# Last batch's attention products on VectorE alone, rows normalized on ScalarE, and loads of rows and expert weights in turn

## The chip, the cores and the metric

The kernel runs on one core of a Trainium2 chip. The metric is the device time of one execution in microseconds. The engines are TensorE (PE: matmuls, with its weight loads PEld), VectorE (DVE), ScalarE (ACT), GpSimd (POOL) and SyncE (SP, which only starts DMAs here). Each takes its instructions in the order in which the program was built, and waits for the others by semaphores.

## The reference

The reference is one layer with cross attention and a mixture of experts, in fp32. B is 4, S 512, the context 1024, D 256, with 16 heads of 16.

```python
x = x + xattn(layernorm(x), ctx, ctx, mask, w_q, w_k, w_v, w_o)   # 16 heads, rope
x = x + ffn(layernorm(x), ln1, ln2, qkv, proj, router, w1, w2)
...
# ffn: hidden_states is (S=256 there, B=4); here dimension 0 has 4 entries and dimension 1 has 512
qkv = einsum('sbh,oh->sbo', ln1_out, qkv_weight)      # 16 query heads, 4 key and value heads
scores = where(causal, einsum('sbhd,tbhd->bhst', q, k) * scale, min)
hidden_after_attn = hidden_states + softmax(scores) @ v @ proj
x = layernorm2(hidden_after_attn)
gate = softmax(x @ router); top_probs, top_idx = top_k(gate, 2)     # of 8 experts
h_mid = gelu(x @ w1[e]); expert_out = h_mid @ w2[e]                 # 256 -> 512 -> 256
out = hidden_after_attn + sum of the two chosen experts, weighted by their gates
```

The second attention runs over the first dimension, which has 4 entries: token t of batch b attends, in each of 16 heads, to token t of batches 0 to b. It is called the inner attention below, and it is no work for matmuls: it is elementwise products with sums over 16 numbers. Batch 3, the last, has the most: four products of q with keys, and four of weights with values.

## The kernel before

**Stages.** Cross attention runs first, batch after batch, in 128 steps of a plan: PE computes scores (L1133 for the maxima, L1154 for the exponentials) and sums (L1172). The second half of the layer is cut into eight halves, `half(b, h)` for batch b and 256 of its 512 tokens. A half is a Python generator: normalization, transposition (L294), q, k, v (psq, L443), inner attention, transposition (psa), projection (psp, L537), residual h2 (L544), second normalization (rows, L557), transposition (psx), router (psl, L569), the choice of two experts (L586 to L608), a placing (psr, L617 to L621: a running count gives each token a row in its expert's table; indices at L638), and four indirect DMAs by POOL (L648) that scatter 2 x 128 rows into `table` in DRAM, twice each. The halves of batches 0 and 1 and most of batch 2 are spread over the plan's steps. What is left of batch 2, and batch 3, run after cross attention, interleaved with the experts.

**Experts.** Tokens are handled in 39 tiles of up to 128 rows of one expert. Lists of tiles are planned as batches become ready: list a has tiles 0 to 8 (after batch 1), b tiles 9 to 16 (after batch 2), c tiles 17 to 25 and d tiles 26 to 38 (after batch 3). A tile needs 128 rows of the table (132.5 KB, SP at L799), its expert's w1 (512 KB, SP at L830, a ring of 8 places, w1 being loaded seven tiles ahead), and w2, which is resident. On PE a tile is psu (16 matmuls, L1432, with a gelu on ScalarE, L1441), psxe (2 transpositions of the next tile's rows, L1414, copied by ScalarE, L1417) and psy (8 matmuls, L1450, copied by ScalarE at L1461). POOL scatters its result (L1464, `given_rows`) once or twice. Where to is computed on VectorE by `gates` (L813 to L820) for a group of a list's tiles: 9 tiles for a, 8 for b, 2 and 7 for c, 13 for d.

**The order after cross attention.** The loop at the end of the kernel goes over the tiles. In round n it emits psu of tile n-1 in two parts, psxe of tile n, and psy of tile n-2 in two parts. Between two of these pieces `others` resumes the generators in `going`: the remaining halves, the plans of lists, the final sums. A generator's `yield "D1.5|G2.4"` tells what it has just emitted: 1.5 us on VectorE beside 2.4 on GpSimd (P, A, D, G are PE, ScalarE, VectorE, GpSimd). `passed` adds that to clocks of the four engines, and the generator is resumed when PE's clock has got to the end of that work (with "!" at the end of the text) or to 2.5 us before. So these texts set the order of all instructions of this stage; no engine departs from it.

**Loads of rows and w1.** `load_list` runs when a list is planned. It goes through all its tiles, and for each tile calls `load_w1` (which issues w1 loads as far as seven tiles beyond the tiles used) and then issues the load of that tile's rows. The first row load of a list waits for the scatters of its batch (`scattered`). After each tile's gelu `load_w1` is called again.

**The last batch's inner attention.** In `half` with b = 3, products alternate: batches 0 and 2 on GpSimd, 1 and 3 on VectorE (L484 for q with keys into `pr`, L509 for weights with values into `pv`); VectorE reduces the scores (L495) and the largest (L496), ScalarE does the exponential (L500) with a change of its function table before it and one back before the next gelu, VectorE sums, divides (L502 to L504) and adds the four products over their batch index by one reduction (L520). For batch 2 the additions are instructions of their own on VectorE (L527).

Of the kernel before, what the change touches and what calls it, by code (L numbers as in the profile page):

```python
# [173 lines left out]
def kernel(  # L174
# [229 lines left out]
    def products_of(name, b):  # L404
        if b < B - 1:
            return k2.tile([P, B - 1, HALF, DK], F32, tag="pr", name=name, bufs=1)
        return late["pool"].tile([P, B, HALF, DK], F32, tag="prlast", name=name, bufs=2)

    def half(b, h):


        n = f"{b}_{h}"
        last = b == B - 1
        mv, *rest = norms_of(b, h)
        yield "D1.7 G1.1"
        both, back, minus = norms_end(b, h, mv, *rest)
        t0 = 2 * h
        if last:
# [17 lines left out]
        if h == 0:  # L436
            keys[b] = keep.tile([P, NQT, KVH * DK], F32, tag=f"keys{b}", name=f"keys{b}")
            values[b] = keep.tile([P, NQT, KVH * DK], F32, tag=f"values{b}", name=f"values{b}")
        q = k2.tile([P, 2, D], F32, tag="q", name=f"q{n}", bufs=1)
        for i in range(2):  # L440
            ps = bank(f"psq{n}_{i}")
            for c in range(KC):
# [23 lines left out]
        def grouped(x):  # L466
            return x.rearrange("p (k r) d -> p k r d", r=REP)

        if b == 0:

            yield
            yield
            yield
            at = k2.tile([P, HALF, DK], F32, tag="at", name=f"at{n}", bufs=1)
            nc.gpsimd.tensor_copy(grouped(at), of_batch(values, 0))
            yield
        else:

            def engine(j):
                return nc.vector if last and j % 2 else nc.gpsimd  # L480

            pr = products_of(f"pr{n}", b)
            for j in range(b + 1):
                engine(j).tensor_tensor(  # L484
                    grouped(pr[:, j]),
                    grouped(q.rearrange("p i (h d) -> p (i h) d", d=DK)),
                    of_batch(keys, j),
                    ALU.mult,
                )
            yield "D1.5|G2.4"  # L490
            sc = k2.tile([P, B, HALF], F32, tag="sc", name=f"sc{n}")[:, 0 : b + 1, :]
            top = k2.tile([P, HALF], F32, tag="top", name=f"top{n}")
            by_head = sc.rearrange("p j n -> p n j")
            over = [P, b + 1, HALF]
            nc.vector.tensor_reduce(sc, pr[:, 0 : b + 1], AX.X, ALU.add)  # L495
            nc.vector.tensor_reduce(top, by_head, AX.X, ALU.max)  # L496
            nc.vector.tensor_tensor(sc, sc, top.unsqueeze(1).to_broadcast(over), ALU.subtract)
            if last:
                yield "D3!"
            nc.scalar.activation(sc, sc, AF.Exp, scale=SCALE)  # L500
            yield "A2.9"
            nc.vector.tensor_reduce(top, by_head, AX.X, ALU.add)  # L502
            nc.vector.reciprocal(top, top)
            nc.vector.tensor_tensor(sc, sc, top.unsqueeze(1).to_broadcast(over), ALU.mult)  # L504
            yield "D1"
            at = k2.tile([P, HALF, DK], F32, tag="at", name=f"at{n}", bufs=1)
            pr = products_of(f"pv{n}", b)
            for j in range(b + 1):
                engine(j).tensor_tensor(  # L509
                    grouped(pr[:, j] if j or last else at),  # L510
                    of_batch(values, j),
                    sc[:, j, :]
                    .rearrange("p (k r) -> p k r", r=REP)
                    .unsqueeze(3)
                    .to_broadcast([P, 2 * KVH, REP, DK]),
                    ALU.mult,
                )
            if last:
                yield "D1.5|G2.4"
                nc.vector.tensor_reduce(  # L520
                    at.rearrange("p n d -> p (n d)"),
                    pr.rearrange("p j n d -> p (n d) j"),
                    AX.X,
                    ALU.add,
                )
            for j in range(1, 1 if last else b + 1):
                (nc.vector if b == 2 else nc.gpsimd).tensor_tensor(at, at, pr[:, j], ALU.add)  # L527
            yield "D2.2!"
        aT = wide(f"aT{n}")
        rows_of = at.rearrange("p (i h) d -> p i (h d)", i=2)  # L530
        transposed(aT, lambda i: rows_of[:, i, :], f"psa{n}")
# [18 lines left out]
        nc.vector.tensor_scalar(v, mv2[:, :, 1], EPS, None, ALU.add)  # L550
        r = power_of(v, 2, "m", f"m{n}")
        nc.gpsimd.tensor_tensor(xt[:, b, t0 : t0 + 2, :], xt[:, b, t0 : t0 + 2, :], h2, ALU.add)
        yield "D1.4 G0.7"
        newton(v, r, 2, "m", f"m{n}")
        rows = k2.tile([P, 2, ROW], F32, tag="rows", name=f"rows{n}")
        for i in range(2):
            nc.vector.tensor_scalar(  # L557
                rows[:, i, 0:D], h2[:, i, :], mv2[:, i, 0:1], r[:, i : i + 1], ALU.subtract, ALU.mult
            )
        yield "D1.4!"  # L560
        xT = wide(f"xT{n}")
        transposed(xT, lambda i: rows[:, i, :], f"psx{n}", 2)
        yield "P0.5 A1.1!"
# [18 lines left out]
        if last:  # L582
            yield "P1 D0.4!"
        nc.scalar.activation(lg, lg, AF.Exp)
        yield "A2.8"
        nc.vector.tensor_reduce(m, lg, AX.X, ALU.add)  # L586
        nc.vector.reciprocal(m, m)
        nc.vector.tensor_tensor(lg, lg, m.to_broadcast(small), ALU.mult)
# [197 lines left out]
    def load_list(name, T, memory):  # L786

        hot, at, beyond = planned["c" if name == "d" else name]
        at0 = FIRST if name == "d" else 0
        of = slice(at0, at0 + T)  # L790
        rows = memory.rearrange("p (t w) -> p t w", w=ROW)
        first, end = {"a": (0, 16), "b": (16, 24), "c": (24, 32), "d": (0, 0)}[name]
        for i in range(T):
            n = at0 + i
            tiles.append((name, i, rows[:, i, :], at[0:1, 1, n : n + 1], at[0:1, 2, n : n + 1]))
            if i:
                load_w1()
            row = nc.sync.value_load(at[0:1, 0, n : n + 1], min_val=0, max_val=E * TOKENS - P)
            inst = nc.sync.dma_start(out=rows[:, i, :], in_=table[bass.ds(row, P), :])  # L799
            if i == 0:  # L800
                after(inst, scattered[first:end])
                load_w1()
        number[name] = memory_of(name, "number", [P, T, 1], I32)
        lists[name] = rows, hot[:, of, :], None if beyond is None else beyond[:, of]

    def gates(name, i0, i1):

        rows, hot, beyond = lists[name]
        of = slice(i0, i1)
        T = i1 - i0  # L810
        g8 = k2.tile([P, LISTS[2] - FIRST, E], F32, tag="g8", name=f"g8{name}{i0}", bufs=1)[:, 0:T, :]
        to = k2.tile([P, LISTS[2] - FIRST], F32, tag="to", name=f"to{name}{i0}", bufs=1)[:, 0:T]
        nc.vector.tensor_tensor(g8, rows[:, of, D : D + E], hot[:, of, :], ALU.mult)  # L813
        nc.vector.tensor_reduce(to, g8, AX.X, ALU.add)
        nc.vector.scalar_tensor_tensor(
            to, to, -float(TOKENS), rows[:, of, D + E], ALU.mult, ALU.add
        )
        if beyond is not None:
            nc.vector.tensor_tensor(to, to, beyond[:, of], ALU.add)
        nc.vector.tensor_copy(number[name][:, of, 0], to)  # L820

    w1_of = []
    used = [0]

    def load_w1():

        while len(w1_of) < len(tiles) and len(w1_of) < used[0] + W1RING - (used[0] > 0):
            expert = nc.sync.value_load(tiles[len(w1_of)][4], min_val=0, max_val=(E - 1) * KC)
            w1_of.append(turn(w1_ring).rearrange("p (c f) -> p c f", f=F))
            nc.sync.dma_start(  # L830
                out=w1_of[-1],
                in_=moe_w1.rearrange("e (c p) f -> p (e c) f", p=P)[:, bass.ds(expert, KC), :],
            )
# [591 lines left out]
    def expert_up(k, part):  # L1425

        if part == 0:
            ps_of[k] = pss.tile([P, F], F32, tag="s", name=f"psu{k}")
        for f in range(2 * part, 2 * part + 2):
            of = slice(f * P, (f + 1) * P)  # L1430
            for c in range(KC):
                nc.tensor.matmul(  # L1432
                    ps_of[k][:, of],
                    w1_of[k][:, c, of],
                    xT_of[k][:, c, :],
                    start=(c == 0),
                    stop=(c == KC - 1),
                )
        if part == 1:
            h_of[k] = turn(h_ring)  # L1440
            nc.scalar.activation(h_of[k], ps_of[k], AF.Gelu_apprx_tanh)  # L1441
            used[0] += 1
            load_w1()

    def expert_down(k, c):
        if c == 0:
# [58 lines left out]
    early = SECOND + EARLY_ALL  # L1505


    ENDS = {"a": (FIRST,), "b": (LISTS[1],), "c": (2, FIRST), "d": (LISTS[2] - FIRST,)}

    def second():  # L1510

# [29 lines left out]


    clock = dict.fromkeys("PADG", 0.0)
    HOP, EARLY = 0.15, 2.5
    going = {}

    def passed(work):

        at = clock["P"]
        for together in work.rstrip("!").split():
            ends = []
            for item in together.split("|"):
                clock[item[0]] = max(clock[item[0]], at) + float(item[1:])
                ends.append(clock[item[0]])
            at = max(ends) + HOP
        return at if work.endswith("!") else at - EARLY

# [137 lines left out]
```

## Time and profile before

| What | Value |
|---|---|
| Runs (3) | 857.05 us median, 854.38 to 857.39 |
| The profiled execution | 852.59 us, span 850.9 us |
| PE busy, share of the span | 802.8 us, 94% |
| VectorE, ScalarE, GpSimd busy | 542.4 us (64%), 454.0 us (53%), 287.9 us (34%) |
| Mean granted clock of PE | 0.984 of full speed |
| Last piece of cross attention (psd, L854) | starts at 640.67 us |
| psxe of tile 17, the first of list c | starts at 737.65 us |
| Last psy (tile 38) | starts at 835.99 us |

Times are microseconds from the start of the span unless "ns" stands there. A line of a list of groups or of a timeline names line, engine, operation, what is written from what, shapes and count. In a timeline the first two numbers are start and duration, merged over the count; brackets hold the idle time of the engine just before, and what ended it. SPq is SP's queue of DMA starts. Matmuls are pipelined, so a busy PE is not a PE at its peak.

### The profile page before, as it was taken

The numbers are of one execution on the slowest core, as the hardware profiler recorded it, in microseconds if no ns is written. First come the engines' busy times: TensorE is split into PE (matmuls) and PEld (weight loads), VectorE is DVE, ScalarE is ACT, GpSimd is POOL, SyncE is SP. The second block draws the span as 40 slices with busy tenths as digits, with TensorE's granted clock in tenths as the row PEclk, the third lists the DMA queues.
The fourth block names the chain that finished last, engine by engine and source line by source line (L and its number), as shares of the span: only waits on it lengthen the run. The fifth ranks groups of instructions, "written<-read, shape, count | busy, mean of one in ns | idle before, by whom it ended". The sixth has DMA issues, their size and how long they took to land.

```text
span 850.9 us, 15007 instructions
## 1 busy us (share of the span) xinstructions
PE 802.8 (94%) x5335; PEld 420.5 (49%) x5335; DVE 542.4 (64%) x1296; ACT 454.0 (53%) x920; POOL 287.9 (34%) x445
## 2 busy tenths in 40 slices
PE   5999999999999999999999999999999979896993
PEld 4553433333443334444334333433337869786993
DVE  5686666766776677886777778888755694400033
ACT  2325656656565655656665565555575654342441
POOL 6815342001353300164562201223213654342531
PEclk9999999999999999999999999999999999997998
DMA  7239101607000000000000023000071451478655
GB/s 231 59 96 308 56 1 58 173 22 208 2 2 1 25 2 1 1 33 20 2 1 1 1 79 120 26 23 6 25 231 62 152 170 41 145 229 305 207 160 164
DMA packets 55642, 73.38 MB, mean 86 GB/s; under 512 B 5721, under 2 KB 40569, under 8 KB 55568
## 3 DMA queue, kind: packets, MB, share of 16 engines
q1 hardware_dynamic: 49968, 61.08, 23.6%
q0 software_dynamic: 4080, 10.07, 3.3%
q10 hardware_dynamic: 1520, 1.27, 0.5%
q8 instruction: 43, 0.70, 0.3%
q14 instruction: 31, 0.25, 0.1%
HBM read 42.88 MB, written 30.75 MB: 87 GB/s over the span
## 4 chain that ended last, share of the span: by engine, by line
PE 72%; issue 9%; DVE 9%; POOL 5%; DMA 2%; ACT 1%; SPq 1%; POOLq 0%; ACTq 0%; DVEq 0%
PE psm L1133 29%; PE av L1172 13%; PE psv L1047 3%; PE psk L1014 3%; POOL given_rows L1464 3%; PE psu L1432 3%; DVE mx L1140 3%; PE pss L1154 2%; PE psq L443 2%; PE psy L1450 2%; PE psp L875 2%; PE psqt L1113 2%; PE pskt L1035 2%; PE psq L1093 2%; PE psp L537 1%
## 5 line engine op out<-in xcount | busy, mean ns | idle before, releaser
L1140 DVE TENSOR_REDUCE mx<-psm 128x1 f32<-128x512 f32 x512 | 326.7, 684 | 133.5 <-PE pss L1154 119.2
L1162 ACT ACTIVATE ex<-pss 128x512 f32<-128x512 f32 x512 | 277.3, 596 | 204.0 <-PE pss L1154 197.0
L1133 PE MATMUL psm<-kT_odd,shared 32*128 32x512 f32 x512 | 152.7, 639 | 1.1 <-DVE mx L1140 0.9
L1154 PE MATMUL pss<-qt,shared 32*128 32x512 f32 x512 | 152.0, 639 | 0.0
L1154 PE MATMUL pss<-qt,kT_odd 32*128 32x512 f32 x512 | 145.9, 644 | 0.5 <-ACT ex L1162 0.5
L1133 PE MATMUL psm<-shared 32*128 32x512 f32 x512 | 144.5, 639 | 1.0 <-ACT shared L1121 0.9
L1172 PE MATMUL av<-ex,vaug 128*32 128x512 f32 (+1 forms) x872 | 106.6, 558 | 0.6 <-ACT oraw L1181 0.6
L1432 PE MATMUL psu<-shared 128*128 128x128 f32 x624 | 81.2, 283 | 11.3 <-DMA shared<-in_moe_w_dram 9.2
L1432 PEld LDWEIGHTS psu<-shared 128*128 128x128 f32 x624 | 78.5, 197 | 15.6 <-issue 9.6
L979 POOL TENSOR_TENSOR shared<-shared 128x256 f32<-128x256 f32 x44 | 33.3, 757 | 140.8 <-ACT shared L1022 108.4
L1133 PEld LDWEIGHTS psm<-kT_odd,shared 32*128 32x128 f32 x512 | 43.8, 183 | 72.3 <-DVE mx L1140 29.4
L1450 PE MATMUL psy<-shared 128*128 x312 | 77.2, 389 | 0.6 <-ACT shared L1461 0.5
L1133 PEld LDWEIGHTS psm<-shared 32*128 32x128 f32 x512 | 43.6, 183 | 66.7 <-DVE mx L1140 27.5
L1450 PEld LDWEIGHTS psy<-shared 128*128 128x128 f32 x312 | 58.0, 197 | 8.7 <-ACT shared L1461 0.9
L1172 PEld LDWEIGHTS av<-ex,vaug 128*32 128x32 f32 x872 | 17.5, 108 | 83.7 <-issue 79.6
L1441 ACT ACTIVATE shared<-psu 128x512 f32<-128x512 f32 x39 | 23.4, 599 | 59.9 <-PE psu L1432 58.1
L1154 PEld LDWEIGHTS pss<-qt,kT_odd 32*128 32x128 f32 x512 | 42.7, 184 | 7.5 <-ACT ex L1162 3.0
L648 POOL DMA_INDIRECT table<-rows,index x32 | 32.4, 1013 | 41.1 <-DVE index L638 23.6
L1496 DVE SCALAR_TENSOR_TENSOR y<-y,gate,xt 128x256 f32<-128x256 f32 x16 | 7.7, 481 | 58.6 <-DMA y<-given_rows 58.6
L981 POOL TENSOR_TENSOR shared<-shared 128x128 f32<-128x128 f32 x88 | 44.6, 528 | 0.0
L1154 PEld LDWEIGHTS pss<-qt,shared 32*128 32x128 f32 x512 | 44.0, 183 | 0.6 <-ACT ex L1162 0.6
L268 POOL TENSOR_TENSOR rm<-vm,power 128x2 f32<-128x2 f32 x8 | 5.7, 712 | 102.2 <-DVE vm L550 102.2
(300 smaller groups left out, 1055.6 us busy)
## 6 DMA issues: line engine op xcount, KB each, us to landing
shared<-in_moe_w_dram SPq DMA_DIRECT2D x47, 512.0 KB, 4.5
table<-zeros SPq DMA_DIRECT2D x8, 2120.0 KB, 17.8
shared<-in_ctxT_dram SPq DMA_DIRECT2D x8, 512.0 KB, 4.2
y<-given_rows SPq DMA_DIRECT2D x12, 256.0 KB, 4.0
shared<-table SPq DMA_DIRECT2D x18, 132.5 KB, 3.6
xt<-in_x_dram SPq DMA_DIRECT2D x4, 512.0 KB, 7.8
rows_d<-table SPq DMA_DIRECT2D x13, 132.5 KB, 2.2
out_dram<-y SPq DMA_DIRECT2D x6, 256.0 KB, 2.2
```

Source lines behind the costliest of these rows:

```text
L648: inst = nc.gpsimd.indirect_dma_start(out=table, out_offset=bass.IndirectOffsetOnAxis(ap=index, axis=0), in_=rows, in_offset=None, bounds_ ...
L979: engine.tensor_tensor(a, src, over(f[:, 0:DK]), ALU.mult)
L981: engine.tensor_tensor(r[:, :, i::2], src[:, :, 1 - i :: 2], over(f[:, DK + i : 2 * DK : 2]), ALU.mult,)
L1014: nc.tensor.matmul(ps[:, 0:D], context(b, kc, c), wk_sb[:, c, :] if b else unpaired(wkp, c), start=(c == 0), stop=(c == KC - 1),)
L1047: nc.tensor.matmul(ps[:, 0:D], context(b, kc, c), wv_sb[:, c, :], start=(c == 0), stop=(c == KC - 1),)
L1133: nc.tensor.matmul(ps, q1[m][rows, t * P : (t + 1) * P], kT[b % 2][rows, g, h * 512 : (h + 1) * 512], start=True, stop=True,)
L1140: nc.vector.tensor_reduce(mx[m][:, t, j, h : h + 1], ps, AX.X, ALU.max)
L1154: nc.tensor.matmul(ps, kT[b % 2][rows, g, kc * P : (kc + 1) * P], q2[m][rows, :], start=True, stop=True,)
L1162: nc.scalar.activation(ex[m, kc, j], ps, AF.Exp, scale=SCALE)
L1172: nc.tensor.matmul(av[m][32 * j : 32 * j + 32, over], vaug[(b * NKC + kc) % VRING][:, 4 * g + j, :], x[:, over], start=(kc == 0), stop=(kc ...
L1432: nc.tensor.matmul(ps_of[k][:, of], w1_of[k][:, c, of], xT_of[k][:, c, :], start=(c == 0), stop=(c == KC - 1),)
L1450: nc.tensor.matmul(ps_of[k], h_of[k][:, f * P : (f + 1) * P], w2_sb[:, bass.ds(weights_of[k] + f * D, D)], start=(f == 0), stop=(f == F // ...
```

## The change

The diff has four parts.

1. In the last batch every product of the inner attention is on VectorE (L484, L509), and the four value products are added by three additions in place of the reduction at L520. The q tile of the last batch has two buffers of its own.
2. The rows of the last batch (L557) are normalized by ScalarE as an activation with scale r and bias -mean x r; VectorE computes that bias.
3. `load_list` puts row loads into a queue `unloaded`; `load_tiles`, in place of `load_w1`, issues before each w1 load one row load (first four tiles of a list other than d) or two. `gates` issues what is missing for its group. The groups of gates are smaller: c in 2, 3 and 4 tiles, d in 4, 4 and 5.
4. The texts of the yields have other durations, and there is a new letter E: ScalarE's work with a table load of 1.3 us ahead of it, and 1.3 us behind it that delay only ScalarE's next work.

```diff
+    def of_half(shape, tag, n, last):
+        if last:
+            return late["pool"].tile(shape, F32, tag=f"{tag}last", name=f"{tag}{n}", bufs=2)
+        return k2.tile(shape, F32, tag=tag, name=f"{tag}{n}", bufs=1)
...
-        yield "D1.7 G1.1"
+        yield "D2 G1.2"
...
-        q = k2.tile([P, 2, D], F32, tag="q", name=f"q{n}", bufs=1)
+        q = of_half([P, 2, D], "q", n, last)
...
-            def engine(j):
-                return nc.vector if last and j % 2 else nc.gpsimd
+            engine = nc.vector if last else nc.gpsimd
...
-                engine(j).tensor_tensor(
+                engine.tensor_tensor(
...
-            yield "D1.5|G2.4"
+            yield "D2.8"
...
-            yield "A2.9"
+            yield "E0.3"
...
-                    grouped(pr[:, j] if j or last else at),
+                    grouped(pr[:, j] if j else at),
...
             if last:
-                yield "D1.5|G2.4"
-                nc.vector.tensor_reduce(
-                    at.rearrange("p n d -> p (n d)"),
-                    pr.rearrange("p j n d -> p (n d) j"),
-                    AX.X,
-                    ALU.add,
-                )
-            for j in range(1, 1 if last else b + 1):
-                (nc.vector if b == 2 else nc.gpsimd).tensor_tensor(at, at, pr[:, j], ALU.add)
-            yield "D2.2!"
+                yield "D2.8"
+            for j in range(1, b + 1):
+                (nc.vector if b >= 2 else nc.gpsimd).tensor_tensor(at, at, pr[:, j], ALU.add)
+            yield "D2.1!"
...
+        if last:
+            away = k2.tile([P, 2], F32, tag="away", name=f"away{n}")
+            nc.vector.scalar_tensor_tensor(away, mv2[:, :, 0], -1.0, r, ALU.mult, ALU.mult)
+            yield "D0.8!"
         for i in range(2):
-            nc.vector.tensor_scalar(
-                rows[:, i, 0:D], h2[:, i, :], mv2[:, i, 0:1], r[:, i : i + 1], ALU.subtract, ALU.mult
-            )
-        yield "D1.4!"
+            of = slice(i, i + 1)
+            if last:
+                nc.scalar.activation(
+                    rows[:, i, 0:D], h2[:, i, :], AF.Identity, bias=away[:, of], scale=r[:, of]
+                )
+            else:
+                nc.vector.tensor_scalar(
+                    rows[:, i, 0:D], h2[:, i, :], mv2[:, i, 0:1], r[:, of], ALU.subtract, ALU.mult
+                )
+        yield "A1.2!"
...
-        yield "A2.8"
+        yield "E0.3"
...
-            if i:
-                load_w1()
-            row = nc.sync.value_load(at[0:1, 0, n : n + 1], min_val=0, max_val=E * TOKENS - P)
-            inst = nc.sync.dma_start(out=rows[:, i, :], in_=table[bass.ds(row, P), :])
-            if i == 0:
-                after(inst, scattered[first:end])
-                load_w1()
+            others_ = scattered[first:end] if i == 0 else ()
+            unloaded.append((name, i, rows[:, i, :], at[0:1, 0, n : n + 1], others_))
         number[name] = memory_of(name, "number", [P, T, 1], I32)
+        load_tiles()
...
+        while any(u[0] == name and u[1] < i1 for u in unloaded):
+            load_row()
...
-    def load_w1():
+    def load_row():
+        name, _, rows, at, others_ = unloaded.pop(0)
+        row = nc.sync.value_load(at, min_val=0, max_val=E * TOKENS - P)
+        inst = nc.sync.dma_start(out=rows, in_=table[bass.ds(row, P), :])
+        after(inst, others_)
+
+    def load_tiles():
 
         while len(w1_of) < len(tiles) and len(w1_of) < used[0] + W1RING - (used[0] > 0):
+            name, i = tiles[len(w1_of)][0:2]
+            for _ in range(1 if name != "d" and i < 4 else 2):
+                if unloaded:
+                    load_row()
             expert = nc.sync.value_load(tiles[len(w1_of)][4], min_val=0, max_val=(E - 1) * KC)
...
-    ENDS = {"a": (FIRST,), "b": (LISTS[1],), "c": (2, FIRST), "d": (LISTS[2] - FIRST,)}
+    ENDS = {"a": (FIRST,), "b": (LISTS[1],), "c": (2, 5, FIRST), "d": (4, 8, LISTS[2] - FIRST)}
...
-    HOP, EARLY = 0.15, 2.5
+    HOP, EARLY, LOAD = 0.15, 2.5, 1.3
...
             for item in together.split("|"):
-                clock[item[0]] = max(clock[item[0]], at) + float(item[1:])
-                ends.append(clock[item[0]])
+                engine, takes = item[0], float(item[1:])
+                if engine == "E":
+
+                    engine, takes = "A", takes + LOAD
+                clock[engine] = max(clock[engine], at) + takes
+                ends.append(clock[engine])
+                if item[0] == "E":
+                    clock[engine] += LOAD
```

More of the change, by code (lines that the diff above doesn't have):

```diff
@@ L508, in half @@
             for j in range(b + 1):
-                engine(j).tensor_tensor(
-                    grouped(pr[:, j] if j or last else at),
+                engine.tensor_tensor(
+                    grouped(pr[:, j] if j else at),
                     of_batch(values, j),
@@ L552, in half @@
         nc.gpsimd.tensor_tensor(xt[:, b, t0 : t0 + 2, :], xt[:, b, t0 : t0 + 2, :], h2, ALU.add)
[L553 removed]
+        yield "D1.4 G0.8"
         newton(v, r, 2, "m", f"m{n}")
         rows = k2.tile([P, 2, ROW], F32, tag="rows", name=f"rows{n}")
+        if last:
+            away = k2.tile([P, 2], F32, tag="away", name=f"away{n}")
+            nc.vector.scalar_tensor_tensor(away, mv2[:, :, 0], -1.0, r, ALU.mult, ALU.mult)
+            yield "D0.8!"
         for i in range(2):
[L557 to L560 removed]
+            of = slice(i, i + 1)
[8 more added lines that the diff above has]
+        yield "A1.2!"
         xT = wide(f"xT{n}")
@@ L820, in gates @@
         nc.vector.tensor_copy(number[name][:, of, 0], to)
-    w1_of = []
+    w1_of, unloaded = [], []
     used = [0]
-    def load_w1():
+    def load_row():
[4 more added lines that the diff above has]
+    def load_tiles():
         while len(w1_of) < len(tiles) and len(w1_of) < used[0] + W1RING - (used[0] > 0):
+            name, i = tiles[len(w1_of)][0:2]
+            for _ in range(1 if name != "d" and i < 4 else 2):
+                if unloaded:
+                    load_row()
             expert = nc.sync.value_load(tiles[len(w1_of)][4], min_val=0, max_val=(E - 1) * KC)
@@ L1442, in expert_up @@
             used[0] += 1
-            load_w1()
+            load_tiles()
     def expert_down(k, c):
```

## The prediction

> **What bounds the kernel now.** I read the page's 40 slices first. TensorE (PE) is at nine tenths nearly everywhere; the weak slices are the last ten, and the granted clock dips there too.
>
> ```profile
> PE   5999999999999999999999999999999979896993
> ...
> PEclk9999999999999999999999999999999999997998
> ```
>
> Then the list of waits, for PE alone from 640 to 840 us, the stage after attention. It says which wait ends last, how long in total, how often, and the longest.
>
> ```profile
> PE psu L1432 <- DMA shared<-in_moe_w_dram: 9.2, 1, 9.2
> PE psa L294 <- DVE at L520: 4.0, 2, 3.0
> PE psxe L1414 <- DMA shared<-table: 2.4, 1, 2.4
> ```
>
> Three things hold PE: one w1 load (9.2), the last batch's inner attention on VectorE (4.0), and the first rows of list c (2.4). The timeline of PE around the largest (start, duration, then in brackets the idle time before it):
>
> ```profile
> 760.15 1.95 PE L1432 MATMUL psu<-shared 128*128 128x128 f32 x16
> 761.94 0.38 PE L1414 MATMUL psxe<-ident,shared 128*128 128x128 f32 x2
> 762.16 1.89 PE L1450 MATMUL psy<-shared 128*128 x8
> 773.28 3.75 PE L1432 MATMUL psu<-shared 128*128 128x128 f32 x16 [9.23 <-DMA shared<-in_moe_w_dram]
> 776.82 0.63 PE L1414 MATMUL psxe<-ident,shared 128*128 128x128 f32 x2
> 777.25 2.52 PE L1450 MATMUL psy<-shared 128*128 x8
> ```
>
> A tile (psu, psxe, psy) recurs every 3.73 us; tile 23's psu, due at 763.9, comes at 773.28, and its round then takes 6.32 instead of 3.73, because the granted clock is 0.50 from 770 to 778 (table of windows). So this hole costs 9.23 + 2.59 = 11.8. Its cause is in the queue of SP:
>
> ```profile
> 735.48 0.34 SPq L799 DMA_DIRECT2D shared<-table  x1
> ...
> 749.10 4.43 SPq L799 DMA_DIRECT2D shared<-table  x4
> 754.31 14.46 SPq L799 DMA_DIRECT2D rows_d<-table  x13
> 769.60 12.35 SPq L830 DMA_DIRECT2D shared<-in_moe_w_dram  x10
> ```
>
> From 749.1 to 768.8 SP issues 17 loads of rows, 1.11 each (14.46/13), that nobody needs yet, and the w1 of tile 23 stands behind them.
>
> **The loads (part one of the change).** The same 22 loads of rows and 22 of w1 are issued for lists c and d, in another order: one row to one w1 for four tiles, then two rows to one w1. A pair costs SP 1.11 + 1.24 = 2.35 (12.35/10 = 1.24 for a w1), a triple 3.46. With row c0 at t, w1 of tiles 17 to 20 are out by t + 9.4, that of tile 23 by t + 19.8; before it was t + 34.1 (735.48 to 769.60). Tile 23's psu is due about t + 28. A triple per 3.73 us is what PE eats, so the lead holds, and the rows are used up at w1 29. The channel carries it: a triple and two result scatters are 512 + 265 + 256 KB per 3.73 us, 277 GB/s; 778 to 782 moved 357. So the hole goes: minus 11.8. What is late next is nothing on SP: the slots of w1's ring fall free 8 tiles earlier. Smaller groups of gates (three more groups of five VectorE instructions at 0.2, 3 us in all) lie in VectorE's idle time. List b's rows now stand between w1 loads that wait for slots; by the walk below the last is out by about 681, VectorE wants them at 693: nothing, and 1 us for each that SP is late beyond that.
>
> **Inner products on VectorE alone.** GpSimd loses 8 products (two groups each of L484 and L509: 3.45, 2.70, 2.50, 2.06, 10.7 us), VectorE gets these 8 and 6 additions, and loses two reductions of L520. Its rows:
>
> ```profile
> 667.84 2.37 DVE L484 TENSOR_TENSOR pr<-q,keys 128x512 f32<-128x512 f32 x2 [0.97 <-ACT q L450]
> ...
> 680.53 3.74 DVE L520 TENSOR_REDUCE at<-pv 128x512 f32<-128x2048 f32 x1 [0.94 <-POOL pv L509]
> 684.18 1.29 DVE L484 TENSOR_TENSOR pr<-q,keys 128x512 f32<-128x512 f32 x2
> ```
>
> The same pair takes 2.37 while GpSimd multiplies (667.89 to 671.34) and 1.29 while it does not: 0.64 alone, 1.19 beside. After the change GpSimd has no products then, so I take 0.64, bounds 0.64 and 1.19. An addition of that size, L527 in batch 2, took 0.69 to 1.53; I take 0.69, the quiet one. A half thus has 2.6 (products) + 2.29 + 0.7, the exponential, 1.05, 2.6 + 2.1, that is 11.3 of VectorE against 16.4 that half 0 took from 667.84 to 684.27, waits and exponential included.
>
> **The order.** The built order of each engine is the same up to tile 1's psu (648.10), and different until psu16; what PE does in between is the same work. On ScalarE the first normalization (L425) moves behind psu4's gelu, from 657.9 to about 665.4; the transposition of attention outputs moves from after psu7 to within psu11 for half 0, from before psu10 to before psu12 for half 1; and the last placing (L617 to L621) from the middle of psu14 to after psy14. So I walk PE forward. From psu1 to the last placing it has 15 psu at 1.78, 15 psxe at 0.22, 15 psy at 1.73, and 18.6 of the last batch (psq 4 x 1.29, L537 2 x 1.73, L875 1.73, three placings 3.0, psx, psl, psa, psh, pso 5.3): with 0.4 for the first psu 75.0, so 723.1 without a wait.
>
> The waits, with the rows named: ScalarE does psxe5's copy behind the normalization (1.08), 0.5. Each exponential costs ScalarE 1.28 + 0.31 + 1.28 ahead of a gelu and the next tile's copy; they stand after psy6 and psy8, and PE waits 0.9 each time before psu9 and psu11. VectorE has half 0's q at 677.3 and half 1's at 678.5: half 0 is scored at 682.9, its sum from 686.5 (ScalarE's place in line, not VectorE's, sets it), output at 696.2, PE asks at 698.3; half 1's output at 702.0, PE asks at 703.4. So VectorE has 2.1 and 1.4 to spare.
>
> **Rows normalized on ScalarE.** VectorE saves 0.86 a half (L557), gets one small instruction (0.16); ScalarE gets two activations, 1.08 by L425, ahead of psu13's copy: 0.5 of wait. A wait is added that the diff does not spell: h2 has one buffer, so half 1's residual (L544) on VectorE must wait until ScalarE has read half 0's h2, 707.0 to 709.0; statistics, GpSimd's power (0.72), a small instruction that takes 1.23 beside GpSimd's addition as now at 691.5, and half 1's rows stand behind it, and psu13's gelu behind those on ScalarE: PE waits 1.0 at half 1's transposition, then 1.1 and 0.3 at the placings, for picks that take 3.05 (L586 to L608). Sum of waits 5.2: the last placing ends at 728.3, against 726.8 before.
>
> Behind it: indices 0.95 (729.2). GpSimd then still has half 0's second two scatters and one result scatter, for their place in line is ahead.
>
> ```profile
> 728.53 0.98 POOL L648 DMA_INDIRECT table<-rows,index  x1 [2.20 <-issue]
> ...
> 732.66 0.97 POOL L648 DMA_INDIRECT table<-rows,index  x1 [0.30 <-issue]
> ```
>
> One costs 1.28 from start to start. Before, four started from 728.53, the last at 732.66; row c0 was issued 2.82 later and PE went on 2.17 after that, at 737.65. After, half 0's come to 730.2, the result scatter to 731.5, half 1's four start 731.8 to 735.65, and PE gets tile 17 at 735.65 + 4.99 = 740.6: plus 2.95. Bounds: 735 if my 5.2 of waits vanish, 747 if each is twice as long and the scatters, 1.26 to 1.34 beside large VectorE operations in two rows here, all pay 0.35. PE's idle time there grows from 2.4 to about 10 us. That wait already left PE slow for 1.6 (psxe 0.69 for 0.38, psy 3.22 for 1.89); the 9.2 wait left 2.59. So 0 to 1.0 more; I take 0.6.
>
> [...] In the trace a table load is 1.28, and around 690 a load, an exponential, a load and a gelu follow each other without a gap (689.40, 690.69, 691.02, 692.31). [...]
>
> **Sum.** Minus 11.8, plus 2.95, plus 0.6: minus 8.3. The profiled execution took 852.59 (span 850.9), so 844.3 by it; the median of the runs shown is 857.05, and from it 848.8. The end, from tile 17 to the output, is otherwise the same 22 rounds.
>
> **Rivals.**
> Waits hidden: ScalarE and VectorE keep up better than my walk, tile 17 comes at 735 (minus 2.65) and the total is minus 14: 843. For: 723.1 is the ledger without waits. Against: five waits have a row each.
> Hole stays: the interleaved loads land late or wait on ring slots, and PE loses in pieces what it lost at once: 854.7 if half of the 11.8 stays, 860.6 if all. This is also the case that the change does not do what it says. For: 778 to 782 ran at a DMA share of 0.98. Against: that was ten w1 back to back.
> Slower: VectorE becomes the bound of the last batch. If products cost 1.19 and additions 1.53, as beside a busy GpSimd, half 0's output is 5.9 later than PE asks, half 1's another 5.4, and in-order ScalarE and PE hand every microsecond on to tile 17. The point from which it decides is 2 us of delay on VectorE; 8.3 beyond that the gain is gone, and at the full price of 11.3 the change is plus 3.0, 860.1; with the scatters' upper price on six of them (2.1) it is 862.2.
>
> **How the numbers follow.** Forecast 0.55, 843 to 855; hidden waits 0.20; hole stays 0.13; VectorE the bound 0.12. Half a per cent, 4.3 us, is about what a measurement of this kernel can tell from no change. Faster by more: nearly all of the first two, 0.73; within: the third and the lower part of the fourth, 0.17; slower by more: the fourth's upper part, 0.10. The range 842 to 857.5 leaves out the fourth case, the late half of the third and a tail of the second.
>
> **What would show it.** Right: no wait of PE for w1 beyond 1 us, psu rounds of 3.73 from tile 18 on; L484's pairs at 1.3; tile 17's psxe at 740 after a wait of 8 to 12 for the table's rows; half 1's residual waiting for ScalarE. Wrong: products over 0.8, PE waiting for at over 2, a w1 wait of several microseconds, or tile 17 before 736 or after 746.

## The result, and the profile after

| | Before | After |
|---|---|---|
| Median of 5 runs each, same chip | 854.38 us | 846.71 us |
| Ratio, 95% interval | | 0.9896 (0.987 to 0.9922) |
| The profiled execution, its span | 852.59, 850.9 | 845.16, 843.4 |
| psd starts | 640.67 | 640.17 |
| psxe of tile 17 starts | 737.65 | 741.70 |
| From there to the end of the span | 113.2 | 101.7 |

The forecast was 848.8 from a reference of 857.05; from the profiled execution before it was 844.3, and the profiled execution after took 845.16. Among the experiments further down are kernels with only some of the four parts, and one of them is 1% faster than the changed kernel.

Line numbers are others in the changed kernel: L484 is L488, L509 is L513, L520 is gone and L525 adds, psu is L1448, psxe L1430, psy L1466, rows L834, w1 L846, the scatters to the table L656, those of results L1480.

The page of the changed kernel, busy tenths of PE and its granted clock in 40 slices:

```profile
PE   5999999999999999999999999999989999789993
...
PEclk9999999999999999999999999999999999889997
```

The 6 of before, where the hole was, is gone, and so is the 7 in slice 33, around the waits at L520. Around the wait for tile 17 stood an 8; now a 7 and an 8 stand there, in slices 35 and 36 (717 to 759 us), and the clock dips. What PE waited for from 640 to 840 us (in total, times, longest):

```profile
PE psxe L1430 <- DMA shared<-table: 8.9, 1, 8.9
PE psu L1448 <- ACT shared L1433: 2.9, 5, 0.6
...
PE psr L625 <- DVE chosen L616: 0.9, 1, 0.9
```

The 9.2 for w1 and the 4.0 for L520 are not there any more. The wait for the first rows of list c has grown from 2.4 to 8.9. The round of tile 23, where the hole was:

```profile
760.75 1.95 PE L1448 MATMUL psu<-shared 128*128 128x128 f32 x16
...
762.75 1.89 PE L1466 MATMUL psy<-shared 128*128 x8
764.48 1.95 PE L1448 MATMUL psu<-shared 128*128 128x128 f32 x16
```

Psu to psu 3.73, no idle time, and in the queue of SP one w1 to two rows:

```profile
759.19 0.38 SPq L846 DMA_DIRECT2D shared<-in_moe_w_dram  x1
760.68 1.31 SPq L834 DMA_DIRECT2D rows_d<-table  x2
762.91 0.38 SPq L846 DMA_DIRECT2D shared<-in_moe_w_dram  x1
```

From 746 to 782 PE is busy all of the time, at a DMA share of 0.89 and 279 GB/s (table of windows). From psu of tile 17 to the end it was 109.40 before and is 97.58: minus 11.82.

The other side of the bill is at tile 17. PE's timeline there:

```profile
723.15 0.39 PE L625 MATMUL psr<-chosen,before 128*128 128x8 f32 x2 [0.94 <-DVE chosen L616]
...
724.28 3.05 PE L1448 MATMUL psu<-shared 128*128 128x128 f32 x16
...
729.75 0.28 PE L625 MATMUL psr<-chosen,before 128*128 128x8 f32 x2
...
741.70 0.66 PE L1430 MATMUL psxe<-ident,shared 128*128 128x128 f32 x2 [8.89 <-DMA shared<-table]
742.50 3.48 PE L1466 MATMUL psy<-shared 128*128 x8
745.82 1.95 PE L1448 MATMUL psu<-shared 128*128 128x128 f32 x16
```

The two placings of the last batch (L625) stand at 723.15 and 729.75. GpSimd's queue, behind the first of them:

```profile
726.15 0.97 POOL L656 DMA_INDIRECT table<-rows,index  x1 [1.70 <-DVE gate L605]
...
731.43 0.97 POOL L1480 DMA_INDIRECT given_rows<-shared,numberb  x1 [0.30 <-DVE place L633]
732.71 0.98 POOL L656 DMA_INDIRECT table<-rows,index  x1 [0.30 <-issue]
...
736.76 0.97 POOL L656 DMA_INDIRECT table<-rows,index  x1 [0.30 <-issue]
```

Nine scatters from 726.15, eight to the table and one of a result, one behind the other. The last half's index was there at 731.86 (L646); before the change the first scatter came 0.79 behind its index, which would be 732.65 here. So the queue (732.71) and PE's last placing are level, and an earlier last placing alone would not have brought row c0 (issued at 739.64) and tile 17 forward.

So the span's minus 7.5 is: the stage starts 0.50 earlier (psd), the way from psd to tile 17 is 101.53 instead of 96.98 (plus 4.55), from psxe to psu of tile 17 4.12 instead of 3.85 (plus 0.27), and minus 11.82.

### The profile page after: what moved, and what is told of

Its sections match the earlier page's. It is cut to its first block, busy times and chain, and to the rows that moved or that the text cites. A ratio compares the mean times of both kernels' runs of the same rounds, so it can differ in the third digit from the quotient of the medians.

```text
span 843.4 us, 15028 instructions
## 1 busy us (share of the span) xinstructions
PE 797.8 (95%) x5335; PEld 417.8 (50%) x5335; DVE 541.7 (64%) x1321; ACT 455.7 (54%) x924; POOL 277.3 (33%) x437
## 3 DMA queue, kind: packets, MB, share of 16 engines
q10 hardware_dynamic: 1520, 1.27, 0.5%
## 4 chain that ended last, share of the span: by engine, by line
PE 72%; issue 10%; DVE 9%; POOL 5%; DMA 2%; ACT 2%; POOLq 0%; SPq 0%; ACTq 0%; DVEq 0%
PE psm L1149 30%; PE av L1188 13%; PE psv L1063 3%; PE psk L1030 3%; POOL given_rows L1480 3%; PE psu L1448 3%; DVE mx L1156 3%; PE psq L448 2%; PE pss L1170 2%; PE psp L891 2%; PE psy L1466 2%; PE psqt L1129 2%; PE pskt L1051 2%; PE psq L1109 2%; PE psp L535 1%
## 5 line engine op out<-in xcount | busy, mean ns | idle before, releaser
L1448 PE MATMUL psu<-shared 128*128 128x128 f32 x624 | 80.0, 279 | 3.2 <-ACT shared L1433 2.9
L1448 PEld LDWEIGHTS psu<-shared 128*128 128x128 f32 x624 | 77.1, 193 | 8.1 <-ACT shared L1433 5.6
L1466 PE MATMUL psy<-shared 128*128 x312 | 76.4, 387 | 0.6 <-ACT shared L1477 0.5
L1466 PEld LDWEIGHTS psy<-shared 128*128 128x128 f32 x312 | 57.8, 195 | 8.2 <-ACT shared L1477 0.9
L656 POOL DMA_INDIRECT table<-rows,index x32 | 32.2, 1006 | 43.5 <-DVE index L646 23.6
```

What stands on the lines that cost most here:

```text
L656: inst = nc.gpsimd.indirect_dma_start(out=table, out_offset=bass.IndirectOffsetOnAxis(ap=index, axis=0), in_=rows, in_offset=None, bounds_ ...
L1448: nc.tensor.matmul(ps_of[k][:, of], w1_of[k][:, c, of], xT_of[k][:, c, :], start=(c == 0), stop=(c == KC - 1),)
L1466: nc.tensor.matmul(ps_of[k], h_of[k][:, f * P : (f + 1) * P], w2_sb[:, bass.ds(weights_of[k] + f * D, D)], start=(f == 0), stop=(f == F // ...
```

## The experiments

Two distances tell most: from psd to psxe of tile 17 (the last batch, then its rows), and from there to the end (the experts). Ratios are to the kernel before, on the chip of the run, with the 95% interval; the distances are from one profiled execution each. The first distance of one kernel can differ by 1 to 3 us between two profiled executions, as the two pairs of repeats show.

| Kernel | Ratio | psd to tile 17 | Tile 17 to end |
|---|---|---|---|
| before | 1 | 96.98 | 113.2 |
| after, first and again | 0.9896 (0.987 to 0.9922), 0.9912 (0.9892 to 0.9932) | 101.53, 103.03 | 101.7, 102.1 |
| loads alone, twice | 0.9874 (0.9851 to 0.9897), 0.9862 (0.9841 to 0.9883) | 99.53, 96.97 | 101.7, 101.1 |
| loads undone | 1.0057 (1.0036 to 1.0079) | 103.24 | 111.4 |
| loads, products on VectorE | 0.9805 (0.9789 to 0.9821) | 92.15 | 101.9 |
| the same and rows on ScalarE (texts of before) | 0.9877 (0.9852 to 0.9902) | 101.10 | 101.9 |
| after, products shared | 0.989 (0.9868 to 0.9913) | 103.64 | 101.7 |
| after, rows on VectorE | 0.9936 (0.9918 to 0.9953) | 105.46 | 101.5 |
| after, h2 of its own | 0.9883 (0.9864 to 0.9901) | 100.03 | 101.8 |

### The loads alone, and the loads undone

To the kernel before, part 3 of the diff alone; from the changed kernel, part 3 alone taken back.

```diff
 # loads alone: before, with
+            unloaded.append((name, i, rows[:, i, :], at[0:1, 0, n : n + 1], others_))
...
-            load_w1()
+            load_tiles()
...
 # loads undone: after, with
-            load_tiles()
+            load_w1()
```

> The kernel before with the new order of row and w1 loads and the smaller groups of gates alone; products, rows and texts of the yields as before, so PE, ScalarE and GpSimd keep their orders. Theory (the hole at tile 23's psu is the loads' alone, and the rest of the change delays tile 17): the wait of 9.2 and the slow round after it go, tile 17's psxe stays near 737.7, span 850.9 - 11.8 = 839, some 1.4% under the kernel before and 4 us under the changed kernel. Rival (the gain is the inner products' and the order's; the loads only move where PE waits): 848 to 851.

> The changed kernel with the loads and groups of gates of before. Theory: the hole comes back at tile 23 with 9 us and a slow round, span 843.4 + 11.8 = 855, slower than the kernel before by the 4 us that tile 17 comes later. Rival (gain from products and order): 843 to 847.

> The loads alone once more, on the chip of the two others: 0.9874 of before in its first measurement, interval 0.9851 to 0.9897. Expected 0.986 to 0.989, psd to tile 17 within 99 to 100, a slow stretch of 1.7 after the wait of 3.0 for L520.

Measured: the loads alone 843.94 us (before 854.24), ratio 0.9874, and on another chip 841.1 (before 852.48), 0.9862; without them the changed kernel takes 858.71, 1.0057. Of PE's waits with the loads undone:

```profile
PE psu L1440 <- DMA shared<-in_moe_w_dram: 8.3, 1, 8.3
```

The wait for w1 is back at 8.3, and behind tile 17 it is 111.4 again. So the loads are worth 1.3% alone and 1.6% inside the change, beside the forecast's 11.8 of 852.59 (1.4%). They carry the whole gain. No run separates the order of the loads from the smaller groups of gates that are in part 3 too; the wait of PE that went is the one for w1. The distances missed what was expected of them: 99.53 where tile 17 was to stay near 737.7, that is at 97, and 96.97 in the repeat, where 99 to 100 was expected. Single profiles of one kernel differ that much. The other three parts together cost 0.6% on the old loads (1.0057), and with the new ones nothing to a few tenths of a per cent: 0.9896 and 0.9912 beside 0.9874 and 0.9862, intervals that overlap.

### The old texts, and products shared again

```diff
 # texts of before: after, with
-            yield "D2.8"
+            yield "D1.5|G2.4"
...
-            yield "E0.3"
+            yield "A2.9"
...
 # products shared: after, with
-            engine = nc.vector if last else nc.gpsimd
+            def engine(j):
+                return nc.vector if last and j % 2 else nc.gpsimd
```

> The changed kernel with the durations in the texts of the yields as before, so that PE has exactly its order of before, with all products on VectorE, rows on ScalarE and the new loads. Theory (the order costs the 4 us, products on VectorE shorten the waits for at, 1.0 and 3.0 before): the waits at psa fall under 1 together, but ScalarE, whose gelu now stands behind the rows, makes PE wait 2 to 3 before psu9; tile 17 at 736 to 738, span 838 to 841. Rival (the products or rows themselves cost, not the order): tile 17 at 741 or later, span 843 or more.

> The changed kernel with the products of batches 0 and 2 on GpSimd again, additions and order as changed. Theory (two engines slow each other: a pair of products takes VectorE 2.4 beside GpSimd and 1.3 alone, so one engine alone is as quick; VectorE had 2 us to spare): scores 1 us later, output of a half 1 to 2 later, PE waits 0 to 2 more, span 843 to 846. Rival (products alone on VectorE are worth several microseconds): span 847 or more. Second rival (GpSimd's help is missed): span under 843.

Measured: 845.28 us (0.9877) and 845.96 (0.989), no difference to the changed kernel that could be told. For the texts of before that is the rival's case (tile 17 at 742.77, span 844.7). With products shared, PE's waits for the last batch's work are no longer than in the changed kernel (psx 1.0, psr 0.3, none at psa; granted clock after them is 0.50 from 718 to 724 and loses 3.4 us, where the changed kernel loses 1.7): so in the new order products on VectorE gain nothing, since PE asks for their sums so late (psa at 698.82 and 704.15 after) that either way is in time.

With the texts of before PE's order is that of the kernel before, and there the rows on ScalarE hurt. ScalarE's timeline of that kernel:

```profile
691.56 0.31 ACT L504 ACTIVATE sc<-sc 128x128 f32<-128x128 f32 x1
694.62 1.09 ACT L560 ACTIVATE rows<-h,away,rm 128x256 f32<-128x256 f32 x2 [2.75 <-POOL xt L550]
695.74 1.28 ACT L1456 ACT_TABLE_LOAD   x1
```

The rows wait 2.75 for statistics that come by way of VectorE, GpSimd and VectorE, and the gelu of a tile whose psu began at 689.68 stands behind them, at 697.03, with its table load. PE waits for both (the profile calls the first of these waits "issue"; it ends when the first row is done), and then runs at a granted clock of 0.50 (697 to 703):

```profile
695.28 0.33 PE L294 MATMUL psx<-ident,rows 128*128 128x128 f32 x1 [1.71 <-issue]
...
698.03 3.78 PE L1447 MATMUL psu<-shared 128*128 128x128 f32 x16 [1.71 <-ACT shared L1432]
```

### The changed kernel again, with an h2 of its own, and with rows on VectorE

```diff
 # h2 of its own: after, with
-        h2 = k2.tile([P, 2, D], F32, tag="h2", name=f"h2{n}", bufs=1)
+        h2 = of_half([P, 2, D], "h2", n, last)
...
-        if last:
-            return late["pool"].tile(shape, F32, tag=f"{tag}last", name=f"{tag}{n}", bufs=2)
+        if last and n.endswith("_1"):
+            return late["pool"].tile(shape, F32, tag=f"{tag}last", name=f"{tag}{n}", bufs=1)
 # rows on VectorE: after, with
-                nc.scalar.activation(
-                    rows[:, i, 0:D], h2[:, i, :], AF.Identity, bias=away[:, of], scale=r[:, of]
+                nc.vector.tensor_scalar(
+                    rows[:, i, 0:D], h2[:, i, :], mv2[:, i, 0:1], r[:, of], ALU.subtract, ALU.mult
...
-        yield "A1.2!"
+        yield "D1.4!"
```

> The changed kernel once more, beside the three others, on one chip. Its own trace: psd 640.17, psxe of tile 17 at 741.70 (101.5 later), psu15 3.05 at 724.28 after waits of 0.78, 0.17 and 0.94, psxe to psu of tile 17 4.12. If these are properties of the built order, psd to tile 17 comes back within 0.5 and psu15 is again about 3; if the slow clock there was an accident of one execution, psu15 is 1.95 and the distance about 100.

> Half 1 of the last batch gets its own q and h2 (half 0 shares those of the other batches); every engine's order is that of the changed kernel. Theory (one buffer of h2 is a wait in the chain): L542 of half 1 no longer waits 1.38 for ScalarE, PE's waits of 0.78 and 0.17 at half 1's transposition go, tile 17 comes 0.95 earlier (distance from psd 100.5). If the short waits are also what lowers the clock at psu15, that psu takes 1.95 and tile 17 comes 2.8 earlier (98.7). Rival: ScalarE's place in line, not h2, sets half 1's rows, and nothing moves (101.5). Either way the time is within 0.4% of the changed kernel's.

> The changed kernel with the last batch's rows normalized on VectorE again, as before (no bias, yield text as before). The scheduler then puts half 1's transposition, router and last placing a good part of a tile earlier. Theory (rows on ScalarE cost 1.0, 1.1 and 0.3 of waits by the h2 buffer and ScalarE's line): tile 17 comes 2 to 3 us earlier, distance from psd 98.5 to 99.5, total 2 to 3 us below the changed kernel. Rival (PE waits instead for VectorE, which now has 1.7 more per pair of halves, or for the choice of experts): distance 101 to 103, no gain.

Measured on one chip (before 855.44): again 848.35 (0.9912), own h2 844.96 (0.9883), rows on VectorE 849.69 (0.9936).

With an h2 of its own the wait of 1.38 at L542 of half 1 and PE's 0.78 and 0.17 are gone, and the distance is 100.03, where 100.5 was expected; the median is 3.4 us under that of the repeat, but the intervals overlap. The slow psu stays without them (3.13, behind a wait of 0.82; granted clock 0.50 from 726 to 728). Rows on VectorE go the rival's way: the scheduler asks for half 1's transposition earlier, PE waits 1.53 there, and 3.4 us are lost behind it at a granted clock of 0.50 (717 to 723); no gain.

The repeat of the changed kernel shows how chance enters. From its timelines of PE and VectorE:

```profile
720.16 1.91 PE L1448 MATMUL psu<-shared 128*128 128x128 f32 x8
...
731.75 0.39 PE L625 MATMUL psr<-chosen,before 128*128 128x8 f32 x2 [0.89 <-DVE chosen L616]
...
732.44 0.59 PE L629 MATMUL psr<-chosen,ones 128*128 128x8 f32 x4
734.60 0.17 DVE L633 TENSOR_TENSOR place<-psr,base 128x16 f32<-128x16 f32 x1 [2.91 <-remote]
```

The instructions, and the waits up to half 1's transposition, are those of the first profile, but the granted clock of 0.50 comes from 719 on, ahead of the first placing, and not behind it at 725. At the end of the last placing that makes no difference: it lies 90.78 behind psd, 90.75 in the first profile, for the wait of 0.94 at the first placing is gone and one of 0.89 stands at the second. The 1.5 us more arise behind it. VectorE takes up the result (L633) 1.57 after the end of the placing, where it was 0.04; GpSimd's queue, never idle for more than 0.31 between its scatters in the first profile, stands idle for 1.26 ahead of the last half's first scatter. The profile names no engine for VectorE's wait ("remote"). The profiles of the loads undone (1.62) and of rows on VectorE (1.57) have the same delay at that line; its cause is open. The length of the stretch at 0.50 varies too: the kernel with 72 extra transpositions, further down, has the same instructions up to them, and there it lost 3.41 instead of 1.7; the last half's first scatter came 94.65 behind psd, and not 92.54.

### Products on VectorE in the old order

The loads alone, with part 1 of the diff (products, additions, buffers of q) and nothing else; PE's, ScalarE's and SP's orders are those of the loads alone.

> The kernel before with the new loads and smaller gate groups, and the last batch's products and additions on VectorE as in the change; rows on VectorE, yield texts and so the orders of PE, ScalarE and SP as before. Theory (the products themselves are a gain, which the change's new order gives back): PE's waits for L520, 1.0 and 3.0 in the run of the loads alone, shrink below 1.0 in sum, the slow stretch of 1.7 behind the longer one goes as well, psd to tile 17 is 95 to 97 where the loads alone had 99.5, and the total is 2.5 to 4.5 below theirs. Rival (VectorE has no slack in this order, and its queue passes the products' time on): distance 99 or more, total the same or above.

Measured: 835.73 us where the loads alone have 841.1 and before 852.48 on the same chip: 0.9805 (0.9789 to 0.9821). It beats both kernels. Waits of PE:

```profile
PE psxe L1422 <- DMA shared<-table: 2.3, 1, 2.3
...
PE psx L294 <- DVE rows L557: 1.3, 1, 1.3
PE psa L294 <- DVE at L525: 1.1, 1, 1.1
```

The 4.0 for the sums has become 1.1, and the granted clock is 1.00 in every window of 1 us between psd and tile 17 (1.7 us lost at 0.50 with the loads alone). The distance is 92.15 instead of 96.97 (92.35 in the profile of the same kernel with 24 transpositions, told next): minus 4.8, and the medians differ by 5.4. That is more than the 2.5 to 4.5 that were expected. So the change had a second gain in it: products on VectorE are worth it, and either of the other two parts, the rows on ScalarE (0.9877 added to this kernel) or the new texts (0.9936 with rows on VectorE), takes it back. The two prices don't add: with both it is 0.9896 to 0.9912.

### The restart behind the wait

72 transpositions of a constant into an unread bank ahead of psxe of tile 17 in the changed kernel; then 24 of them in the kernel just told. They are extra work whose result nobody reads.

```diff
     def expert_x(k):
         x = tiles[k][2]
+        if k == FIRST + LISTS[1]:
+            warm = pss.tile([P, F], F32, tag="s", name="warm")
+            for _ in range(72):
+                nc.tensor.transpose(warm[:, 0:P], ident, ident)
```

> The changed kernel with 72 extra transpositions of a constant into an unread bank, put on PE just ahead of the psxe of tile 17: dummy work that fills the wait of 8.89 for the table's rows. Nothing else differs. Theory (the restart after that wait is slow because the granted clock fell during it): psxe takes 0.38 and psy 1.89 (0.66 and 3.48 in the changed kernel), psxe to psu of tile 17 2.3 in place of 4.12, total 1.6 to 1.9 below. Rival (the restart is slow because operands or banks come late): 4.1 stays and the total is the same, or later if the 72 last longer than the wait.

> The same with 24 extra transpositions of a constant into an unread bank ahead of the psxe of tile 17 (dummy work). With 72 of them the psxe and psy after the wait took 0.38 and 1.89 in place of 0.66 and 3.48, but the burst ended some 5 us after the rows could have been there. 24 took 2.7 in one piece, which is less than the 3.1 that PE waits with the loads alone. Theory (granted clock): psxe to psu of tile 17 2.0 to 2.4 where about 4 is usual, total 1.5 to 2 below the kernel without them. Rival (the burst is followed by pauses of 1 us, or the clock falls anyway): same or later.

With 72 the total is 849.31 us (0.9926): the burst was too long. Its end, and the restart:

```profile
744.61 6.25 PE L1431 MATMUL warm<-ident 128*128 128x128 f32 x41 [1.00 <-issue]
750.70 0.38 PE L1434 MATMUL psxe<-ident,shared 128*128 128x128 f32 x2
...
752.64 1.95 PE L1452 MATMUL psu<-shared 128*128 128x128 f32 x16
```

After 25 transpositions in 2.9 us came pauses of 0.45, 0.99, 0.99 and 1.00, of whose cause the profile says only "issue", and then a granted clock of 0.50 to 0.53 from 745 to 748 within the burst itself. But psxe to psu of tile 17 is 1.94 instead of 4.12, at a granted clock of 1.00 from 750 to 754 where the changed kernel had 0.50 from 741 to 745: the slow restart is the clock. With 24 it is 2.78 (2.0 to 2.4 was expected) and the next psu 2.02, beside 3.22 and 2.99 in the kernel without them. These 1.4 us do not show in the total (836.54, 0.9817), which is no lower.

## Why the prediction was right, and where its sum was off

**The hole** (minus 11.8): measured minus 11.82, and the two experiments on the loads show it to be theirs. The queue of SP, the ring and the channel behaved as worked out (279 GB/s, 277 forecast), and PE does not wait for a w1 at all: the rival that the hole stays fell.

**Products and additions**: 0.64 and 0.69 forecast, 0.63 and 0.71 measured when no GpSimd product runs. The groups of VectorE from 660 to 710 (x8 has both halves; end to end, the merged timeline gives 2.50 for four products):

```profile
L488 DVE TENSOR_TENSOR pr<-q,keys 128x512 f32<-128x512 f32 x8 | 5.0, 685 | 12.3 <-ACT q L455 12.3
L525 DVE TENSOR_TENSOR at<-at,pv 128x512 f32<-128x512 f32 x6 | 4.1, 688 | 0.1
```

The rival that VectorE becomes the bound fell with that.

**The table loads**: 1.28 each, as in the trace of before. At 685.31, 686.60, 686.93 and 688.22 a load of 1.28, the exponential, a load of 1.28 and the gelu follow each other, with no idle time listed between them.

**Tile 17** (plus 2.95): this is the term that was mis-sized; psd to tile 17 grew by 4.55. The steps of the walk, from psu1 (647.60) to the end of the last placing (730.92), 83.3 in all:

- "75.0, so 723.1 without a wait" was too little. Without waits and without the slow stretch it was 77.8. In the mean of 15 a psu took 1.88 from start to start, not 1.78, and a psy 1.82, not 1.73 (waits and the slow stretch taken off). The psu of 1.78 are there; but one that begins behind a wait took 2.02 (those at 647.60, 659.27, 689.22 and 697.70).
- The slow clock was left out. From 725 to 729 the granted clock is 0.50 to 0.76, 1.7 us of it lost: psu15 takes 3.05, psxe 0.64, psy 2.36. The trace of before has the same loss, from 703 to 707 behind the wait of 3.0 for L520, and I had counted a slow clock only behind the two long waits (9.2 and 2.4 before).
- "Sum of waits 5.2" was too much: 3.9. The copy behind the normalization (0.58 for 0.5), half 1's transposition (0.95 for 1.0) and the first placing (0.94 for 1.1) are there as told, and L542 waits 1.38 for L561; the exponentials cost 0.61 each instead of 0.9, and the waits at psu13 and the second placing are not there.

That makes the last placing end at 730.9 where 728.3 was forecast, 3.1 later counted from psd. In the forecast GpSimd's queue hid 1.8 of lateness there (index 729.2, with 0.8 behind it 730.0, and the queue free at 731.8); what was over, 1.4, shows at half 1's first scatter, though the queue, begun late itself, was free no sooner. The rest is one scatter of 1.49 instead of 1.28; from the last scatter to PE it was 4.94 (forecast 4.99).

**The restart** (plus 0.6): plus 0.27, of a slow restart that was there before as well (psxe to psu of tile 17 3.85 before, 4.12 after).

**Luck in the number.** The total is nearer than its parts: the term for tile 17 was 1.6 too small, the one for the restart 0.3 too large, and psd came 0.5 earlier, by chance (from 640.17 to 643.65 in the thirteen profiles). In the repeat of the changed kernel the distance to tile 17 is 1.5 longer still. And 848.8 started from the median of three runs, 857.05; from the 854.38 of five the same minus 8.3 gives 846.1, beside 846.71 measured.

**What the forecast did not ask.** It added the parts up and never asked what each would do in the others' absence. It saw the products only as a way to be in time for the new order; the run of loads and products shows that in the old order they save 4.8 us.

What remains open: why the first distance of one kernel differs by up to 2.6 us between two profiles (96.97 and 99.53 with the loads alone). In the longer one PE has a wait of 1.1 at the q matmuls that the profile only calls "issue", and the last placing ends 1.46 later; then row c0 is issued 4.54 behind the last scatter to the table instead of 2.76, and PE goes on 1.54 behind that instead of 2.22. The half clock isn't the cause, its loss is 1.7 in both. Nor do the runs separate the new texts from each other.

## What to carry to other kernels

When a change has several parts, find the stage that each one acts on and price each alone: here a reordering of loads was the whole gain, and a good part was hidden by an order and a move that cost as much. In an in-order engine an instruction that waits for a long chain must not be put ahead of work that others need now, even if its own engine has time for it: with rows on ScalarE and the texts of before the rows waited 2.75 ahead of a gelu, and PE waited 1.71 twice. Count a short wait of TensorE with what the clock may do behind it: nothing, or 1.7 or 3.4 us lost at a granted clock of 0.50 here. And do not read a difference of 1 or 2 us between two kernels from one profile of each.

## What the runs showed of the hardware

**Half clock, 1.7 or 3.4 us at a time.** In windows of 1 us from psd to the last psu ahead of tile 17, the clock granted is 1.00, but for one stretch of 0.50 that loses 1.7 or 3.4 us, in every profile but the two of loads with products, which lose nothing. It comes behind waits, of 0.94 in the changed kernel and of 3.0 before, but not behind all: waits of 1.28 and 1.15 in the run of loads with products left the clock at 1.00. In the repeat of the changed kernel two waits of 0.80 and 0.16 were all the idle time listed in the 11 us ahead of it. In one execution of that kernel the stretch begins at 719 and in another at 725; why was not shown.

**VectorE beside GpSimd.** With products shared, in one execution: a pair of products 2.37 while GpSimd multiplies (678.28) and 1.29 while it doesn't (684.76); three additions 3.05 beside a GpSimd product (701.47) and 2.21 without one (693.70).

**One queue's rhythm.** Indirect scatters that follow each other on GpSimd start 1.27 to 1.30 apart in every run, and now and then 1.34 to 1.58. In the changed kernel nine in a row are 10.6 us from the first start to the last (726.15 to 736.76).
